# Key projections of two blocks ahead of the values, and the softmax ahead of the first group's row work, in a cross-attention and expert kernel

## Chip, cores and metric

The kernel runs on one core of one Trainium2 chip. The metric is the device time of one execution in microseconds (us); smaller is better. In what follows PE is the matrix engine, DVE the vector engine, ACT the scalar engine, POOL the GpSimd engine and SP the engine whose queue issues nearly all DMA transfers.

## The reference

```python
x = x + xattn(layernorm(x), ctx[:, :100], ctx[:, :100])      # 32 batches of 100 rows, width 512, 16 heads of 32, causal
x = x + ffn(layernorm(x))
# xattn: q = X WQ^T, k = C WK^T, v = C WV^T; softmax(q k^T / sqrt(32)) v; times Wfc^T, plus bfc
# ffn: shared expert  gelu(x Ws_g^T) * (x Ws_u^T) Ws_d^T  over all 3200 rows, plus 16 experts,
#      each with the 12 best rows of each batch (top_k of softmax(x gate_w^T)), scaled and scattered back
```

Only the first 100 context rows of a batch matter, since the mask is causal. All is float32. Each float32 operand is split into a rounded high part and a low rest, and one product is three matmuls (high by high, high by low, low by high); `mm3` issues them.

## The kernel before

The 3200 rows lie in order of batch. **Keys and values** are projected in nine blocks j of 2, 2, 3, 3 ... tiles of 128 rows. `kproj(j, c)` gives the keys of a block for one quarter c of the width in 12 matmuls, `kkeep` copies them from PSUM to a ring of SBUF tiles on ACT (L200) and stores them to DRAM from SP (L201). `vproj(j, i)` gives the values of one tile, `vkeep` copies and stores them (L183, L185). Both projections use one PSUM ring of two tiles (`ps_kv`, which `qproj` and later the first group's matmuls use too), so a projection waits until the last but one result has been copied out. The SBUF ring `kk` has two tiles, so a copy waits until the last but one store has landed.

**The prologue** is written out by hand: loads of the weights of keys (four `split_wc(0, c)`), values (`split_w(1, d)`) and queries (`split_wc(2, c)`), of the context of blocks 0, 1 and 2 (`ctx_load`, `ctx_split`), and of four tiles of x with their layer norm (`x_load`, `x_stats`, `x_norm`) and their transposes on PE (`x_turn`). Each split is a cast on ACT (L100, L134) and a subtraction on DVE or POOL (L101, L135). Its order on PE is: four keys of block 0, two values of block 0, first key of block 1, `x_turn`, three keys of block 1, first value of block 1.

**The units.** 32 units follow, one for each quarter of the width of four batches. Unit u projects q (`qproj`), takes the scores and softmax of unit u - 1 (`scores`, `sm_max` on DVE, `sm_sub` on POOL, `sm_exp` on ACT, `sm_sum` on DVE, `sm_mul` on POOL), and turns the probabilities of unit u - 2 on PE (`p_turn`, L277, copied by `p_keep`, L282) and multiplies them by the values (`values`, L292, copied by `y_keep`). `p_turn`, `values`, `x_turn` and `turn` share a second PSUM ring of two tiles (`ps_ms`). In most units one more key and value tile is projected.

**The last three units** (`end` = 0, 1, 2, that is units 29, 30 and 31) have no keys and values left. In their place stands the row work of the feed-forward's first group of three tiles (class `Prep`): `split_y` (ACT L826, DVE L827), `fc` (12 matmuls), `bias` (L837), `add` (L846), `stats`, `rsqrt` on POOL (L859, L860), `norm`, `turn` (four transposes, L885) and `logits`. `F.chunk_load` loads a chunk of expert weights (768 KB, L615) into a ring of two raw tiles, and `chunk_split` splits it (ACT L626, DVE L627); the chunk 0 is split in three parts. Then come the tail (scores, softmax, transposes and values of the last unit) and `F.begin`, the first gate and up matmuls of the shared expert, and the long feed-forward stage.

On each engine the order of instructions is that of the program's text within the hand-ordered region. Where that region meets the feed-forward's, a scheduler merges both, so the order there is read from the built program: in the tail ACT casts the last part of chunk 0, then takes the second `sm_exp`, then casts chunk 1, then does the first two `p_keep`, then casts chunk 2, then does the other two.

Of the kernel before, what the change touches and what calls it, by code (L numbers as in the profile page):

```python
# [11 lines left out]
ALU = mybir.AluOpType  # L12
# [6 lines left out]
NC4 = D // 128  # L19
# [7 lines left out]
KMAX = 384  # L27
KS = 1
FC_AT = 9
BUF = dict(cr=4, raw=6, cx=8, x=5, v=2, kk=2, kt=3, vt=2, q=3, p=5, pt=5, y=2, pj=2, sc=1, tr=2)  # L30
GROUPS = [3, 2, 2, 3, 3, 3, 3, 3, 3]
GMAX = 384
NSLOT = B * CAP
# [6 lines left out]
def f32(ap):  # L40
    return ap.bitcast(F32)
# [18 lines left out]
def attention(tc, K, F):  # L60
    nc = tc.nc
    with ExitStack() as ctx, ExitStack() as kvctx:
# [40 lines left out]
        def load_w(w, dk):  # L103
            r = raw.tile([128, D], F32, name="raw")
            nc.sync.dma_start(r, K.wA[w, :, dk, :])
            return r

        def split_w(w, dk, r):
            split(WH[w][:, dk, :], WL[w][:, dk, :], r)

        def load_wc(w, c):
            r = raw.tile([128, D], F32, name="raw")
            nc.sync.dma_start(r.rearrange("p (d n) -> p d n", d=NC4),
                              K.wA[w, :, :, c * 128:(c + 1) * 128])
            return r

        def split_wc(w, c, r, eng=None):
            cs = slice(c * 128, (c + 1) * 128)
            split(WH[w][:, :, cs], WL[w][:, :, cs], r.rearrange("p (d n) -> p d n", d=NC4), eng)
# [3 lines left out]
        def ctx_load(j, d):  # L123
            t0, n = KSTART[j] * 128, KVB[j] * 128
            cr = crp.tile([128, KMAX], F32, name="cr")
            nc.sync.dma_start(cr[:, 0:n], K.ctxT[d, :, t0:t0 + n])
            cur["cr", j, d] = cr
# [11 lines left out]
        def x_load(sb, b):  # L139
            if b == 0:  # L140
                cur["xh", sb] = xnp[sb % 2].tile([128, NC4, SB], FR, name="xnh")
                cur["xl", sb] = xnp[sb % 2].tile([128, NC4, SB], FR, name="xnl")
            xt = xp.tile([S, D], F32, name="xt")
            r0 = (sb * 4 + b) * S
            nc.sync.dma_start(xt, K.x[r0:r0 + S, :])
            cur["x", sb, b] = xt

        def x_stats(sb, b):
            st = stp.tile([S, 6], F32, name="bst")
            mv = stp.tile([S, 2], F32, name="mv")  # L150
            rs = stp.tile([S, 1], F32, name="rs")
            nc.vector.bn_stats(st, cur["x", sb, b])
            nc.vector.bn_aggr(mv, st)
            nc.gpsimd.tensor_scalar(rs, mv[:, 1:2], EPS, None, ALU.add)
            nc.gpsimd.tensor_tensor(rs, rs, K.nhalf[0:S, 0:1], ALU.pow)
            cur["mv", sb, b] = mv, rs
# [40 lines left out]
        def kkeep(j, c, pk):  # L197
            t0, n = KSTART[j] * 128, KVB[j] * 128
            kk = kkp.tile([128, KMAX], F32, name="kk")
            nc.scalar.copy(kk[:, 0:n], pk[:, 0:n])  # L200
            nc.sync.dma_start(K.kD[:, c, t0:t0 + n], kk[:, 0:n])  # L201
# [104 lines left out]
        def prologue():  # L306
            nc.gpsimd.dma_start(mask, K.mask)
            wk = [load_wc(0, 0)]
            for d in range(NC4):
                ctx_load(0, d)  # L310
            wk += [load_wc(0, c) for c in range(1, NC4)]
            wv = [load_w(1, 0), load_w(1, 1)]
            split_wc(0, 0, wk[0])
            for d in range(NC4):
                ctx_split(0, d, nc.vector)
            wv.append(load_w(1, 2))
            for b in range(2):
                x_load(0, b)
            p0 = kproj(0, 0)
            split_wc(0, 1, wk[1])  # L320
            wv.append(load_w(1, 3))
            kkeep(0, 0, p0)
            p0 = kproj(0, 1)
            split_wc(0, 2, wk[2])
            split_wc(0, 3, wk[3])
            for b in range(2, 4):
                x_load(0, b)
            for d in range(NC4):
                ctx_load(1, d)
            wq = [load_wc(2, 0), load_wc(2, 1)]  # L330
            kkeep(0, 1, p0)
            p0 = kproj(0, 2)
            split_w(1, 0, wv[0])
            split_w(1, 1, wv[1])
            kkeep(0, 2, p0)
            p0 = kproj(0, 3)
            split_w(1, 2, wv[2])
            x_stats(0, 0)
            split_w(1, 3, wv[3])
            wq += [load_wc(2, 2), load_wc(2, 3)]  # L340
            kkeep(0, 3, p0)
            p0 = vproj(0, 0)
            x_norm(0, 0)
            x_stats(0, 1)
            x_stats(0, 2)
            x_norm(0, 1)
            x_stats(0, 3)
            for d in range(NC4):
                ctx_split(1, d, nc.vector)
            x_norm(0, 2)  # L350
            x_norm(0, 3)
            vkeep(0, 0, p0)
            p0 = vproj(0, 1)
            split_wc(2, 0, wq[0])
            for d in range(NC4):
                ctx_load(2, d)
            x_load(1, 0)
            vkeep(0, 1, p0)
            for c in range(NC4):
                kkeep(1, c, kproj(1, c))  # L360
                if c == 0:
                    for b in range(4):
                        x_turn(0, b)
                if c:
                    split_wc(2, c, wq[c], nc.gpsimd)
                    ctx_split(2, c - 1)
                else:
                    kload(0)
            ctx_load(3, 0)
            vkeep(1, 0, vproj(1, 0))  # L370

        with tc.manual_schedule():
            prologue()
            for u in range(NU):
# [26 lines left out]
                if end == 0:  # L401
                    F.chunk_load()
                    F.chunk_load()
                if end == 1:
                    pr.add(0)
                    pr.stats(0)
                    pr.rsqrt(0)
                if end == 2:
                    pr.add(2)
                    pr.stats(2)  # L410
                    pr.rsqrt(1)
                    pr.store(0)
                if a is not None:
# [8 lines left out]
                if end == 0:  # L422
                    pr.bias(0)
                if end == 1:
                    pr.bias(1)
                if end == 2:
                    pr.rsqrt(2)
                if mine:
                    qkeep(u, qproj(u))
                if a is not None:  # L430
                    sm_exp(a, 0)
                if end == 0:
                    pr.split_y(0)
                if back is not None:
                    p_turn(back, 0)
                    p_turn(back, 1)
# [1 line left out]
                    p_keep(back, 1)  # L438
                if xs:
                    x_stats(sb + 1, c)  # L440
                if end == 0:
                    pr.split_y(1)
                if end == 2:
                    pr.norm(1)
                if a is not None:
                    sm_exp(a, 1)
                    sm_sum(a, 0)
# [3 lines left out]
                if end == 1:  # L451
                    pr.fc(1)
                    pr.norm(0)
                    F.chunk_split(0, 0)
                if end == 2:
                    pr.turn(0)
                    pr.norm(2)
                if mine and c == 1:
                    vload(sb)
                if back is not None:  # L460
# [7 lines left out]
                    sm_sum(a, 1)  # L468
                    sm_mul(a, 1)
                if end == 0:  # L470
                    pr.split_y(2)
                if end == 1:
                    pr.bias(2, nc.vector)
                    pr.add(1)
                    pr.stats(1)
                if mine and jn in blocks:
# [11 lines left out]
                if end == 1:  # L488
                    pr.fc(2)
                if end == 2:  # L490
                    F.chunk_split(0, 1)
                    pr.turn(1)
                if back is not None:
                    values(back)
                if end == -1:
# [14 lines left out]
            for b in range(4):  # L510
                p_turn(last - 1, b)
                p_keep(last - 1, b)
            pr.turn(2)
            values(last - 1)
            for hb in range(2):
                sm_exp(last, hb)
                sm_sum(last, hb)
                sm_mul(last, hb)
                if hb == 0:
                    y_keep(last - 1)  # L520
                    pr.logits()
                    F.chunk_split(0, 2)
            pr.store(2)
            F.chunk_split(1)
            scctx.close()
            F.open_gu()
            F.begin(pr.done())
            pr.tokens()
            for b in range(4):
                p_turn(last, b)  # L530
                p_keep(last, b)
            F.begun()
            values(last)
            y_keep(last)
# [2 lines left out]
class FeedForward:  # L537
# [77 lines left out]
            self.nc.sync.dma_start(self.raws[n], self.K.wE[n // NFC, n % NFC])  # L615
            self.asked += 1

    def chunk_split(self, n, part=None):
        nc, f = self.nc, n % NFC
        if n not in self.sw:  # L620
            hl = self.wp[f].tile([128, 2, 3 * D], FR, name=f"whl{f}")
            self.sw[n] = hl[:, 0, :], hl[:, 1, :]
        h, l = self.sw[n]
        r = self.raws[n]
        cs = slice(0, 3 * D) if part is None else slice(part * D, (part + 1) * D)
        nc.scalar.copy(h[:, cs], r[:, cs])  # L626
        nc.vector.tensor_tensor(l[:, cs], r[:, cs], f32(h[:, cs]), ALU.subtract)  # L627
        if part in (None, 2):
            self.chunk_load()

# [421 lines left out]
```

## Time and profile before

| what | value |
|---|---|
| time of one execution | 1749.06 us median of 3 (1748.99 to 1749.1) |
| the profiled execution | 1750.64 us, its span from first to last instruction 1748.8 us |
| mean granted PE clock | 0.987 |
| busy in the span | PE 1698.7 us, DVE 885.7, ACT 681.2, POOL 445.0 |
| 0 to 41 us (prologue) | PE busy 32.1 us of 41 |
| 41 to 330 us (units to 27) | PE busy 277.4 us of 289, clock 0.98 |
| 330 to 385 us (units 28 to 31) | PE busy 47.2 us of 55, clock 0.88 |
| 385 to 400 us (tail) | PE busy 13.0 us of 15, clock 0.89 |
| 400 to 1740 us (feed-forward) | PE busy 1329 us of 1340, clock 1.00 |

Times of single instructions below are in microseconds from the span's start. In a timeline line the first number is the start, the second the duration of the group; `x4` counts its instructions, and the bracket says how long the engine had sat idle before and what released it. A line of the windows gives a stretch, its length, the busy time of PE with its number of matmuls, the granted clock (1.00 is full, 0.50 half), and the load of the DMA engines.

### The profile page before, as it was taken

What the parts mean: (1) busy time and instruction counts of PE and PEld (TensorE: products, weight loads), DVE (VectorE), ACT (ScalarE), POOL (GpSimd) and SP (SyncE); (2) the same over time, 40 slices, a digit from 0 to 9 for tenths busy, and PEclk for the clock granted to TensorE, in tenths of its full rate; (3) what the DMA queues carried; (4) which work ended last, traced back from release to release, by engine and by line L of the source; (5) the groups of instructions that cost most, each with busy time, mean ns of one, the idle gap of its engine ahead of it and who ended that gap; (6) DMA issues with size and microseconds to landing.
All of it is one profiled execution on the core that took longest, in us unless ns stands there. A gap on an engine that the chain in (4) does not pass through costs nothing.

```text
span 1748.8 us, 27994 instructions
## 1 busy us (share of the span) xinstructions
PE 1698.7 (97%) x11072; PEld 1559.6 (89%) x11072; DVE 885.7 (51%) x2118; ACT 681.2 (39%) x1086; POOL 445.0 (25%) x399
## 2 busy tenths in 40 slices
PE   7999999989999999999999999999999999999996
PEld 6888888878888999999889999999999999999996
DVE  4877777775333333333454444444444444444431
ACT  4555555543112111211234444444444444444431
POOL 3777777661111011101020111110111111011111
PEclk9999999989999999999999999999999999999998
DMA  7444443534111101102154555554555554555531
GB/s 211 136 137 155 131 131 118 164 109 134 70 63 59 55 31 67 61 19 73 46 185 142 163 141 153 158 158 148 148 159 147 163 153 143 156 162 137 137 88 18
DMA packets 82995, 211.13 MB, mean 121 GB/s; under 512 B 9489, under 2 KB 35842, under 8 KB 82864
## 3 DMA queue, kind: packets, MB, share of 16 engines
q1 hardware_dynamic: 71792, 183.87, 32.2%
q0 software_dynamic: 10784, 25.21, 7.9%
q8 instruction: 87, 1.43, 0.3%
q14 instruction: 44, 0.36, 0.1%
q10 hardware_dynamic: 288, 0.27, 0.0%
HBM read 163.71 MB, written 45.60 MB: 120 GB/s over the span
## 4 chain that ended last, share of the span: by engine, by line
PE 91%; DVE 3%; DMA 2%; POOL 2%; ACT 1%; issue 1%; SPq 0%; POOLq 0%; ACTq 0%; DVEq 0%
PE gu L55 46%; PE dn L55 23%; PE kv L55 10%; PE m L55 3%; PE ms L277 2%; PE sc L236 2%; PE ms L292 1%; POOL p L256 1%; DMA big<-yD 1%; PE m L779 1%; DVE p L247 1%; PE ms L167 1%; DVE xt L161 1%; DMA kD<-kk 1%; PE m L894 1%
## 5 line engine op out<-in xcount | busy, mean ns | idle before, releaser
L55 PE MATMUL gu<-xh,whl 128*128 128x384 f32 (+1 forms) x3200 | 645.0, 333 | 1.3 <-ACT g L654 1.3
L55 PEld LDWEIGHTS gu<-xh,whl 128*128 128x128 f32 x3200 | 559.0, 188 | 18.8 <-ACT g L654 1.5
L55 PE MATMUL dn<-whl,hh 128*128 128x512 f32 x1168 | 372.4, 400 | 0.0
L627 DVE TENSOR_TENSOR whl<-wraw,whl 128x1536 fp32r<-128x1536 f32 (+1 forms) x138 | 242.1, 1755 | 241.9 <-ACT whl L626 241.8
L55 PE MATMUL gu<-xl,whl 128*128 128x384 f32 (+1 forms) x1600 | 338.1, 333 | 0.0
L55 PEld LDWEIGHTS gu<-xl,whl 128*128 128x128 f32 x1600 | 280.8, 188 | 0.0
L655 DVE TENSOR_TENSOR g<-g,gu 128x384 f32<-128x384 f32 (+1 forms) x200 | 108.7, 544 | 319.1 <-PE gu L55 316.8
L658 ACT CAST hh<-g 128x384 fp32r<-128x384 f32 (+1 forms) x200 | 100.9, 505 | 431.8 <-DVE g L655 431.8
L55 PEld LDWEIGHTS dn<-whl,hh 128*128 128x128 f32 x1168 | 213.3, 189 | 37.3
L626 ACT CAST whl<-wraw 128x1536 fp32r<-128x1536 f32 (+1 forms) x138 | 201.4, 1460 | 105.3 <-PE dn L55 103.4
L55 PE MATMUL dn<-whl,hl 128*128 128x512 f32 x584 | 230.9, 395 | 0.0
L654 ACT ACTIVATE g<-gu 128x384 f32<-128x384 f32 (+1 forms) x200 | 96.7, 484 | 312.5 <-PE gu L55 312.4
L793 POOL DMA_INDIRECT out_dram<-x,isl x48 | 77.5, 1615 | 365.5 <-ACT x L792 355.8
L659 DVE TENSOR_TENSOR hl<-g,hh 128x384 fp32r<-128x384 f32 (+1 forms) x200 | 111.8, 559 | 114.2 <-ACT hh L658 114.2
L768 POOL DMA_INDIRECT big<-xnD,isl x48 | 48.7, 1015 | 422.5 <-PE m L779 351.8
L55 PEld LDWEIGHTS dn<-whl,hl 128*128 128x128 f32 x584 | 109.8, 188 | 25.9
L271 POOL TENSOR_TENSOR p<-p,sm 100x800 f32<-100x800 f32 x64 | 101.2, 1583 | 51.0 <-DVE sm L266 36.6
L256 POOL TENSOR_TENSOR p<-p,mx 100x800 f32<-100x800 f32 x64 | 96.5, 1528 | 49.7 <-DVE mx L247 49.7
L837 POOL TENSOR_TENSOR x<-x,bfc 128x512 f32<-128x512 f32 x24 | 44.4, 1875 | 248.4 <-DMA x<-x 248.4
L247 DVE CUSTOM_DVE_ANT_0 p<-sc,mask 100x100 f32<-100x100 f32 x512 | 95.6, 257 | 16.6 <-PE sc L236 16.6
L265 DVE TENSOR_REDUCE sm<-p 100x8 f32<-100x800 f32 x64 | 62.7, 980 | 14.1 <-ACT p L260 14.1
L260 ACT ACTIVATE p<-p 100x800 f32<-100x800 f32 x64 | 56.2, 879 | 17.3 <-POOL p L256 17.3
(138 smaller groups left out, 1650.7 us busy)
## 6 DMA issues: line engine op xcount, KB each, us to landing
wraw<-wE SPq DMA_DIRECT2D x136, 768.0 KB, 4.5
xt<-x SPq DMA_DIRECT2D x32, 200.0 KB
vD<-vt SPq DMA_DIRECT2D x25, 256.0 KB, 2.1
kt<-kD SPq DMA_DIRECT2D x32, 200.0 KB, 4.9
v<-vD SPq DMA_DIRECT2D x8, 800.0 KB
x<-x SPq DMA_DIRECT2D x25, 256.0 KB, 5.1
xnD<-xn SPq DMA_DIRECT2D x25, 256.0 KB, 2.0
out_dram<-x SPq DMA_DIRECT2D x25, 256.0 KB, 2.2
```

Of the source, the lines that this page charges most:

```text
L55: r = nc.tensor.matmul(out, t[0][a], t[1][b], start=(first and i == 0), stop=(last and i == n - 1))
L247: nc.vector.tensor_tensor_reduce(out=p[:, bb, h, :], in0=sc[:, h, cs], in1=mask, scale=ISCALE, scalar=NEG, op0=ALU.add, op1=ALU.max, accum ...
L256: nc.gpsimd.tensor_tensor(pv, pv, mx[:, :, None].to_broadcast([S, 8, S]), ALU.subtract)
L265: nc.vector.tensor_reduce(sm, pv, AX.X, ALU.add)
L271: nc.gpsimd.tensor_tensor(pv, pv, sm[:, :, None].to_broadcast([S, 8, S]), ALU.mult)
L626: nc.scalar.copy(h[:, cs], r[:, cs])
L627: nc.vector.tensor_tensor(l[:, cs], r[:, cs], f32(h[:, cs]), ALU.subtract)
L654: nc.scalar.activation(g[:, 0:t], pg[:, 0:t], AF.Gelu)
L655: nc.vector.tensor_tensor(g[:, 0:t], g[:, 0:t], pu[:, 0:t], ALU.mult)
L658: nc.scalar.copy(hh[:, 0:t], g[:, 0:t])
L659: nc.vector.tensor_tensor(hl[:, 0:t], g[:, 0:t], f32(hh[:, 0:t]), ALU.subtract)
L793: ins = nc.gpsimd.indirect_dma_start(out=self.K.out, out_offset=bass.IndirectOffsetOnAxis(ap=r.isl[:, i:i + 1], axis=0), in_=o, in_offset= ...
```

## The change

It has three parts. **Rings:** the key copies get a ring of four tiles instead of two, the loaded key tiles (`kt`) two instead of three. **Prologue:** PE does the four keys of block 0, the four keys of block 1, the two values of block 0, `x_turn`, the first value of block 1. To that end the context of block 1 is loaded ahead of the last two value weights and of all x tiles, and its split stands beside the keys of block 0; the x tiles are loaded behind the second key store; the splits of the value weights and the statistics of x stand between the keys of block 1. One of the three context splits of block 2 in the prologue goes from POOL to DVE.

**Last units and tail:** in units 30 and 31 the softmax's maxima come ahead of `add`, `stats` and `rsqrt` of tiles 0 and 2; the three `split_y` move behind the softmax and the transposes of unit 29; `bias(2)` goes from DVE to POOL; the splits of chunk 0's first two parts move from units 30 and 31 to unit 31 and the tail, with their subtractions on POOL; `logits` goes behind `F.begin`; the split of chunk 1 goes behind the last unit's transposes.

In the built program the merged order in the tail is a different one: ACT casts the last part of chunk 0, then chunk 2, then copies the logits, then does the four `p_keep` of the last unit, and then casts chunk 1.

```diff
-BUF = dict(cr=4, raw=6, cx=8, x=5, v=2, kk=2, kt=3, vt=2, q=3, p=5, pt=5, y=2, pj=2, sc=1, tr=2)
+BUF = dict(cr=4, raw=6, cx=8, x=5, v=2, kk=4, kt=2, vt=2, q=3, p=5, pt=5, y=2, pj=2, sc=1, tr=2)
...
-            wv.append(load_w(1, 2))
-            for b in range(2):
-                x_load(0, b)
+            for d in range(NC4):
+                ctx_load(1, d)
             p0 = kproj(0, 0)
             split_wc(0, 1, wk[1])
-            wv.append(load_w(1, 3))
+            wv.append(load_w(1, 2))
             kkeep(0, 0, p0)
             p0 = kproj(0, 1)
             split_wc(0, 2, wk[2])
-            split_wc(0, 3, wk[3])
-            for b in range(2, 4):
-                x_load(0, b)
-            for d in range(NC4):
-                ctx_load(1, d)
-            wq = [load_wc(2, 0), load_wc(2, 1)]
+            wv.append(load_w(1, 3))
             kkeep(0, 1, p0)
             p0 = kproj(0, 2)
-            split_w(1, 0, wv[0])
-            split_w(1, 1, wv[1])
+            split_wc(0, 3, wk[3])
+            for b in range(4):
+                x_load(0, b)
+            wq = [load_wc(2, 0), load_wc(2, 1)]
+            ctx_split(1, 0, nc.vector)
             kkeep(0, 2, p0)
             p0 = kproj(0, 3)
...
+            for d in range(1, NC4):
+                ctx_split(1, d, nc.vector)
             kkeep(0, 3, p0)
+            for c in range(NC4):
+                p0 = kproj(1, c)
+                split_w(1, c, wv[c])
+                kkeep(1, c, p0)
+                if c == 0:
+                    wq.append(load_wc(2, 2))
+                    kload(0)
+                if c == 1:
+                    wq.append(load_wc(2, 3))
+                x_stats(0, c)
+                if c:
+                    x_norm(0, c - 1)
...
             vkeep(0, 1, p0)
-            for c in range(NC4):
-                kkeep(1, c, kproj(1, c))
...
+            for b in range(4):
+                x_turn(0, b)
             ctx_load(3, 0)
-            vkeep(1, 0, vproj(1, 0))
+            p0 = vproj(1, 0)
+            for d in range(NC4 - 1):
+                ctx_split(2, d, nc.vector if d == 0 else nc.gpsimd)
...
                 if end == 1:
+                    pr.add(0)
+                    pr.stats(0)
+                    pr.rsqrt(0)
                     pr.bias(1)
                 if end == 2:
+                    pr.add(2)
+                    pr.stats(2)
                     pr.rsqrt(2)
...
                 if end == 0:
-                    pr.split_y(2)
+                    for i in range(pr.nt):
+                        pr.split_y(i)
                 if end == 1:
-                    pr.bias(2, nc.vector)
+                    pr.bias(2)
...
+            y_keep(last - 1)
+            F.chunk_split(0, 2)
             pr.store(2)
-            F.chunk_split(1)
             scctx.close()
             F.open_gu()
             F.begin(pr.done())
+            p_turn(last, 0)
+            p_turn(last, 1)
+            pr.logits()
...
             pr.tokens()
-            for b in range(4):
-                p_turn(last, b)
-                p_keep(last, b)
+            F.chunk_split(1)
             F.begun()
```

## The prediction, made before the changed kernel was run

> **What bounds the kernel now.** I read the page first, then the waits of PE, then stretches of one clock step each, then the timelines of ACT and SP in the two places that the change touches.
>
> ```profile
> PE 1698.7 (97%) x11072; PEld 1559.6 (89%) x11072; DVE 885.7 (51%) x2118; ACT 681.2 (39%) x1086; POOL 445.0 (25%) x399
> ...
> PE 91%; DVE 3%; DMA 2%; POOL 2%; ACT 1%; issue 1%; SPq 0%; POOLq 0%; ACTq 0%; DVEq 0%
> ```
>
> PE is busy for 97% of the span and makes 91% of the chain that ended last. The change adds and removes no matmul. So its whole effect is the time in which PE waits, and the time in which PE runs at half clock. The waits of PE over the span name what can be won:
>
> ```profile
> PE ms L167 <- DVE xt L161: 10.4, 7, 1.7
> ...
> PE ms L277 <- ACT pt L282: 4.1, 3, 2.3
> PE ms L885 <- ACT pt L282: 3.7, 1, 3.7
> ...
> PE kv L55 <- ACT kk L200: 3.0, 2, 2.2
> ```
>
> The last is the prologue's key ring (2.2 us and 0.7 us). The second and third lie in units 29 to 31. The first is `x_turn` in units without a value tile; nothing here touches it. ACT's own rows in the prologue show why the key copies are late: the store two tiles back had not landed.
>
> ```profile
> 15.66 0.37 ACT L200 COPY kk<-kv 128x256 f32<-128x256 f32 x1 [2.50 <-DMA kD<-kk]
> 20.99 0.37 ACT L200 COPY kk<-kv 128x256 f32<-128x256 f32 x1 [3.92 <-DMA kD<-kk]
> ```
>
> The windows, cut where the clock changes, show what an idle gap costs beside itself:
>
> ```profile
> 78.38:81.79 3.41, 1.82 (x58) 1.00 0.57 180
> 81.79:85.21 3.42, 3.42 (x28) 0.50 0.33 120
> ...
> 341.20:344.62 3.42, 2.17 (x17) 1.00 1.03 355
> 344.62:348.03 3.41, 2.34 (x15) 1.00 1.04 320
> ...
> 365.10:368.51 3.41, 0.91 (x10) 1.00 0.00 0
> 368.51:371.92 3.41, 1.78 (x8) 0.50 0.20 77
> 371.92:375.34 3.42, 3.22 (x44) 0.50 0.00 0
> ```
>
> After a window of 3.41 us with 1.82 us busy (1.90 at 252.46), the next runs at half clock; 2.17 and 2.34 busy kept it full. At half clock a 128x512 matmul takes 0.425 us instead of 0.23, so a half window of dense work costs 1.6 us. Units 30 and 31 and the tail have five such windows (368.51 to 382.16, and 395.82 to 399.23).
>
> **Part 1, the prologue.** Before, `qproj` of unit 0 starts at 35.38. Now, in turn:
> - The fourth key ends at 13.84, as before: it waits for nothing that moves by more than 0.1.
> - Block 1's context now follows the second value weight (cast at 12.54, after waiting for its landing). Between the two key stores that ACT waited for, SP's queue moved two x tiles, four context tiles, two query weights and a store, 1552 KB, in 20.9 - 15.6 = 5.3 us, so 290 KB per us. 512 KB then land by 14.3; with a cast of 0.41 and a subtraction of 0.42, key 5 runs from 14.0 to 15.7 with a short stall. The wait of 2.2 us is gone, and the half clock behind it (16.94 to 20.35, 1.6 us).
> - Keys 6 to 8, at 1.44 each (12 matmuls, 29.74 to 31.18): 20.0.
> - The first value needs key 7's PSUM tile copied, and that copy needs the *third* key store landed. The x tiles and two query weights now stand ahead of that store on SP. Counted up, 4768 KB are queued up to and with it; up to the second store before it were 4640 KB of the same transfers, landed at 20.9. So it lands at 21.4, the copy ends at 21.7, and PE has idled 1.7 us. A ring of four takes away one wait and moves the other.
> - Two values at 2.76 (32.62 to 35.38) end at 27.2, four `x_turn` at 2.5 together (25.71 to 28.23, their own stall included) at 29.7, the value of block 1 at 32.5. That is 2.9 us earlier. If the 1.7 us fall into one window, half clock takes back 1.6; if the store lands 1 us later as well, 0.3 is left. I take half a chance of half clock: **-2.1**, between -2.9 and -0.3.
>
> On SP the x loads move behind two stores; they land by 20, and the last norm is done before `x_turn` at 27. SP still stands at `kt` until key 5's store has landed (4.7 us before); what queues behind it is block 2's context, needed at 41. The smaller `kt` ring costs nothing: its slot is read by the scores of the unit before, done when SP comes there. DVE's extra 128x384 split (at most 1.0, POOL's row at L135) lies beside `vproj`.
>
> **Part 2, units 1 to 28.** Nothing is edited, but the 1.65 us idles at `x_turn` shift against the clock's windows. Four of six (78, 164, 209, 252 us) now lie inside one window and cost 1.5 each. Shifted, it may be two to six: -3 to +3, taken as **0**.
>
> **Part 3, units 29 to 31, against before's times.** In unit 29 ACT now does exp (343.61), two `p_keep` (0.87), exp (345.2), two `p_keep`, and only then `split_y`: the first cast ends at 347.3 where it ended at 345.2. `fc(0)` starts at 347.45 instead of 346.33, and PE has idled 3.2 us instead of 2.3 inside some 4 us. That drops one of the two windows above under 1.82, so half clock follows, 1.2 to 1.6. The `yl` subtractions, hidden then as now, are done before `fc` needs them. In unit 30 `fc(1)` waits 0.85 us, since `add(0)`, which frees its PSUM tile, now stands behind 16 maxima (2.96 us). Against that, unit 31's maxima no longer wait for `bias`, two `add` and `stats`: they start at 365.0 to 365.4, before at 365.19. So the gain in the softmax pays for what unit 29 lost. `turn(0)` starts at 369.5 to 369.9 (369.70 before), the second gap of 1.8 us follows (the PSUM slot waits for `turn(0)`'s subtraction), and the half clock over transposes, scores and values stays as it was. The last part of chunk 0 is split 0.3 to 0.6 earlier than before; were the clock to stay full, the same steps give 381.3 instead of 386.06, so -4.7. POOL's two new subtractions (1.29 each, its row for 128x512 at L101) and `bias(2)` (1.29 to 1.57) stand behind both `sm_sub` or end 2 us before the next: nothing.
>
> **Part 4, the tail,** decides. When chunk 0's last part is split, SP issues chunk 2's load into its slot:
>
> ```profile
> 386.06 0.33 SPq L615 DMA_DIRECT2D wraw<-wE  x1
> ...
> 390.90 1.48 ACT L626 CAST whl<-wraw 128x1536 fp32r<-128x1536 f32 x1 [0.97 <-DMA wraw<-wE]
> ```
>
> From that issue to ACT's cast of chunk 2 it is 4.84 us, and to the first `dn` matmul (398.37) 12.3 us, with chunk 1 cast before. Now that cast stands on ACT ahead of the logits' copy, the four `p_keep` and chunk 1's cast, and all these wait for the load: 4.84, cast 1.38, copy 0.38, first `p_keep` 0.49 give 7.1; two more transposes at half clock (0.8 each) and `p_keep` give 9.3; chunk 1's cast 1.47 gives 10.7; then 24 matmuls, 4.2 at full clock or 7.7 at half, since PE has idled 4 us before. So 15 to 18 us, 16.0 taken. With the issue at 385.7 `dn` starts at 401.7: **+3.3** (-1 where the clock had stayed full, +5 at worst). The next chunk's loads come 8 us later than before but are needed only at 408.
>
> [...]
>
> **Sum.** -2.1 + 0 + 3.3 = +1.2. The profiled execution took 1750.64 (1.84 outside its span), 1.58 over the median of 1749.06; the difference is the same on either, so 1750.3 on the median. About 0.2%, 3.5 us, is what a measurement of this kernel can tell from no change.
>
> **Rivals.**
> - *No measurable change* (the forecast, 0.50): gain in the prologue, given back in the tail: 1746 to 1752.5. It holds the case that the rings don't do what they are for: if the third store lands at 23.5, the prologue gives 0 and the time is 1752.4.
> - *Slower* (0.29): ACT's queue behind chunk 2's load. The wait is there whatever the clock does, 3.7 us by the middle of its range, 5.5 with half clock through all 24 matmuls. It decides when issue to `dn` passes 16.5 us with a prologue of -0.3, or 18.3 with -2.1 (12.3 + 3.5 + the prologue's gain + 0.4 for the earlier issue). Price: -0.3 + 4.8, 1753.6. For it: ACT's order in the built program. Against: two of its terms rest on a half clock.
> - *Faster* (0.21): the gap of 3.69 us before `turn(0)` goes, the clock stays full from unit 29 to the tail, `dn` starts at 381.3 + 16 = 397.3 (-1.1), the prologue gives -2.9, and one idle less is punished in the loop (-1.5): 1743.6. Against: unit 29 idles more than now.
>
> The range of 8 in 10 reaches from the faster case, 1744.0, to a little over the slower one, 1754.5.
>
> **What would show it.** Right: `qproj` of unit 0 near 32.5, a key copy waiting for a store at about 21, a gap of 3 us in unit 29, ACT idle for about 4 us before chunk 2's cast, and issue to `dn` near 16. Wrong: a clock of 1.00 from 340 to 380, or chunk 1's cast ahead of chunk 2's.

## The result and the profile after

The changed kernel takes 1753.73 us (median of 20 runs, 1749.37 to 1755.08), the kernel before, run beside it, 1749.14 us (20 runs, 1747.22 to 1751.38). The ratio is 1.0024, with a 95% interval of 1.0017 to 1.0031: some 4 us slower, on the edge of the 0.2% that can be told from no change. A second measurement, told below, gave 1.0014 (1.0003 to 1.0025). That the change is slower is settled; whether by more or by less than 0.2% is not.

The time lies inside the predicted range and 3.4 us above the predicted value. It is outside the forecast of no measurable change (1746 to 1752.5), and it is the time of the rival "slower" (1753.6).

The profiled execution after took 1753.64 us (span 1751.9), the one before 1750.64 (span 1748.8), so 3.0 us of the 4.6 between the medians can be looked up in the two traces. The other 1.6 is that the profiled execution of before was itself 1.5 over its median.

From the page of the changed kernel, the busy times and the chain that ended last:

```profile
PE 1697.2 (97%) x11072; PEld 1558.3 (89%) x11072; DVE 884.3 (50%) x2116; ACT 680.5 (39%) x1086; POOL 445.9 (25%) x401
...
PE 90%; DVE 2%; POOL 2%; DMA 2%; issue 1%; ACT 1%; SPq 0%; POOLq 0%; ACTq 0%; DVEq 0%
```

PE has the same 11072 matmuls and still makes 90% of the chain. The difference is in its waits. In the list of PE's waits over the span (total, times, longest) two lines matter:

```profile
PE ms L277 <- issue: 5.0, 1, 5.0
...
PE kv L55 <- ACT kk L200: 2.6, 1, 2.6
```

The second is the key ring: before it was two waits of 2.2 and 0.7, now it is one of 2.6. It stands ahead of the first value, where ACT waits for a key store before it copies the seventh key (a row of ACT's timeline, then one of PE's):

```profile
22.10 0.37 ACT L200 COPY kk<-kv 128x256 f32<-128x256 f32 x1 [4.03 <-DMA kD<-kk]
22.52 0.50 PE L55 MATMUL kv<-wh,cxh 128*128 128x512 f32 x1 [2.56 <-ACT kk L200]
```

The first is new. "issue" means that the profile found no semaphore for it; what it is shows on ACT. ACT's timeline in the tail (start, duration, and in brackets the idle time and its releaser):

```profile
383.04 0.62 ACT L622 CAST whl<-wraw 128x512 fp32r<-128x512 f32 x1
390.29 1.47 ACT L622 CAST whl<-wraw 128x1536 fp32r<-128x1536 f32 x1 [6.63 <-DMA wraw<-wE]
391.78 0.47 ACT L893 COPY so<-kv 16x384 f32<-16x384 f32 x1
392.28 0.89 ACT L282 COPY pt<-ms 100x400 f32<-100x400 f32 x2
```

ACT stands 6.63 us in front of chunk 2's cast. The load that it waits for could not be issued before DVE had done its last subtraction of chunk 0 (rows of DVE and of SP's queue):

```profile
384.26 1.21 DVE L623 TENSOR_TENSOR whl<-wraw,whl 128x512 fp32r<-128x512 f32 x1
385.53 0.33 SPq L611 DMA_DIRECT2D wraw<-wE  x1
```

Behind chunk 2's cast in ACT's queue are the copy of the logits and the first two `p_keep`, whose inputs PE had finished by 387.84 and 386.4. They start at 391.78 and 392.28 in these rows, behind the end of that cast at 391.76. The next two transposes need the PSUM tiles that `p_keep` frees, so PE stands too. PE's timeline:

```profile
386.98 0.86 PE L890 MATMUL kv<-xl,gw 128*64 128x384 f32 x4
392.87 1.54 PE L277 MATMUL ms<-ident,p 100*100 100x100 f32 x8 [5.03 <-issue]
...
401.71 0.63 PE L55 MATMUL dn<-whl,hh 128*128 128x512 f32 x2
```

Half clock is on record behind these gaps. In the windows of 3.41 us, cut at the clock's steps (stretch, length, PE's busy time and matmuls, granted clock, DMA share, GB/s) a whole window is empty in the tail, and two of half clock come after it; after 2.37 us of idle in unit 29 comes one:

```profile
344.03:347.45 3.42, 1.04 (x9) 1.00 1.05 417
347.45:350.86 3.41, 3.41 (x9) 0.50 0.92 322
...
388.41:391.82 3.41, 0.00 (x0) 1.00 0.50 199
391.82:395.23 3.41, 2.36 (x23) 0.50 0.16 20
395.23:398.65 3.42, 3.33 (x35) 0.50 0.53 215
```

The two traces, stretch by stretch. "T" is the first matmul behind the transposes and values of unit 30: that of the logits before (382.41), that of the gate after (381.28). From T to the first `dn` both kernels do the same PE work in another order.

| stretch | before | after | difference |
|---|---|---|---|
| start to `qproj` of unit 0 | 35.38 | 35.22 | -0.16 |
| to the scores of unit 1 | 14.53 | 15.06 | +0.53 |
| to the scores of unit 28 | 289.43 | 288.95 | -0.48 |
| unit 29, to the scores of unit 29 | 10.78 | 13.40 | +2.62 |
| unit 30, to the scores of unit 30 | 11.31 | 12.00 | +0.69 |
| unit 31, to T | 20.98 | 16.65 | -4.33 |
| T to the first `dn` | 15.96 | 20.43 | +4.47 |
| first `dn` to the last matmul's end | 1336.78 | 1336.51 | -0.27 |

The half clock falls elsewhere in each execution (from 345 to 385 us the mean clock was 0.83 in `before`, 0.87 in `after`, and 1.00 in `after_again`, which has the text of `after`), so the profiled executions of the runs below are needed beside this pair. The tail's loss holds in them: T to the first `dn` takes 19.2 to 21.3 us in the five executions that have the order of the changed tail (this one, `c_only`, `store34`, `y_early`, `after_again`), and 16.0 to 16.7 in the three that have the order of before (`before`, `p_only`, `ring_only`). The sum of the units and the tail spreads more: from the scores of unit 28 to `dn` it is 59.5 to 63.3 us in the four executions with the changed last units and tail (without `y_early`), and 57.9 to 60.0 in three with those of before.

### The profile page after: what moved, and what is told of

It reads as the page before. It is cut to its first block, busy times and chain, and to the rows that moved or that the text cites. A ratio compares the mean times of both kernels' runs of the same rounds, so it can differ in the third digit from the quotient of the medians.

```text
span 1751.9 us, 27984 instructions
## 1 busy us (share of the span) xinstructions
PE 1697.2 (97%) x11072; PEld 1558.3 (89%) x11072; DVE 884.3 (50%) x2116; ACT 680.5 (39%) x1086; POOL 445.9 (25%) x401
## 4 chain that ended last, share of the span: by engine, by line
PE 90%; DVE 2%; POOL 2%; DMA 2%; issue 1%; ACT 1%; SPq 0%; POOLq 0%; ACTq 0%; DVEq 0%
PE gu L55 46%; PE dn L55 23%; PE kv L55 9%; PE m L55 4%; PE ms L277 2%; PE sc L236 2%; POOL p L256 2%; PE ms L292 1%; PE m L775 1%; DVE p L247 1%; DVE xt L161 1%; PE ms L167 1%; DMA big<-yD 1%; PE m L890 1%; PE m L881 1%
## 5 line engine op out<-in xcount | busy, mean ns | idle before, releaser
L277 PE MATMUL ms<-ident,p 100*100 100x100 f32 x512 | 56.7, 254 | 10.1 <-issue 5.0
```

Of the source, the lines that this page charges most:

```text
L277: nc.tensor.transpose(tp[0:S, h, 0:S], p[:, b % 2, h, :], K.ident[0:S, 0:S])
```

## The experiments

All ratios are to the kernel before, run in the same batch (its medians were 1750.07, 1750.79 and 1750.10 in the three batches).

| run | median us (n) | ratio (95%) |
|---|---|---|
| `p_only` | 1749.74 (11) | 0.9991 (0.9982 to 1.0000) |
| `c_only` | 1753.37 (11) | 1.0017 (1.0008 to 1.0026) |
| `a_hook` | 1752.24 (11) | 1.0008 (0.9999 to 1.0017) |
| `store34` | 1751.64 (11) | 1.0006 (0.9996 to 1.0016) |
| `a_hook2` | 1751.84 (12) | 1.0005 (0.9993 to 1.0018) |
| `y_early` | 1750.69 (12) | 1.0000 (0.9991 to 1.0010) |
| `best2` | 1743.68 (7) | 0.9967 (0.9954 to 0.9979) |
| `best3` | 1746.83 (12) | 0.9979 (0.9970 to 0.9987) |
| `ring_only` | 1746.60 (8) | 0.9979 (0.9969 to 0.9989) |
| `t_hook2` | 1747.35 (12) | 0.9993 (0.9979 to 1.0007) |
| `best4` | 1743.35 (6) | 0.9971 (0.9959 to 0.9983) |
| `after_again` | 1753.21 (9) | 1.0014 (1.0003 to 1.0025) |

**The halves alone.** `p_only` is the kernel before with the change's `BUF` line and its whole `prologue()`:

```diff
-BUF = dict(cr=4, raw=6, cx=8, x=5, v=2, kk=2, kt=3, ...
+BUF = dict(cr=4, raw=6, cx=8, x=5, v=2, kk=4, kt=2, ...
...
```

> The kernel before with the change's rings and prologue alone; units 29 to 31 and the tail as before. Theory of the tail (the slowdown is ACT's queue held by chunk 2's load between begin and the first dn): the prologue gives nothing, because the third key store lands at 22 and half clock follows, and unit 0 loses 0.5 more at x_turn; qproj of unit 0 starts at 35.2, the scores of unit 0 at 41.3, time within 1 us of the kernel before (1748.5 to 1750.1). Rival (the prologue shifts the loop's idles against the clock's windows, so that more of them are punished, and that is most of the 4.6 us): 1752 or more.

`c_only` is the changed kernel with the line and the prologue of before:

```diff
-BUF = dict(cr=4, raw=6, cx=8, x=5, v=2, kk=4, kt=2, ...
+BUF = dict(cr=4, raw=6, cx=8, x=5, v=2, kk=2, kt=3, ...
...
```

> The changed kernel with the rings and the prologue of before; units 29 to 31 and the tail of the changed kernel. Theory of the tail: nearly all of the loss is here, 1752.5 to 1754; from the load of chunk 2 to the first dn 16 us. Rival (prologue and clock windows carry the loss): 1749 to 1751.

The first gave -0.09%, the second +0.17%. In the trace of `p_only`, `qproj` of unit 0 starts at 35.56 and the scores of unit 0 at 41.61 (35.38 and 40.77 before). In that of `c_only`, from the load of chunk 2 (385.34) to the first `dn` (401.69) it is 16.35 us. So the loss is in the last units and the tail, and the prologue is not what slows the kernel. (The profiled execution of `p_only` was the slowest of its eleven, 3.1 us over their median; the times, not its trace, carry this.)

**The whole once more**, to see whether the halves add up:

> The changed kernel once more, beside the other three on one chip. The parts run alone gave -0.09% for the prologue and +0.17% for units 29 to 31 with the tail, together +0.08%, and the whole +0.24%. If the two parts are separate, this run comes near +0.1% (1.0005 to 1.0016); if they make each other worse, near +0.24% again (1.0018 or more).

It gave +0.14%. This lies in the band for separate parts, but its interval (0.03 to 0.25) holds both cases; whether the two halves make each other worse stays open.

**ACT's order.** `a_hook` moves chunk 2's split of the first feed-forward job from behind job step 0 to a hook that `hidden` calls after its gelu:

```diff
         nc.scalar.activation(g[:, 0:t], pg[:, 0:t], AF.Gelu)
+        if hook:
+            hook()
...
             if g == 0:
-                for f in range(NFC - 2):
+                self.hook = lambda: self.chunk_split(2)
+                for f in range(1, NFC - 2):
```

> The changed kernel, and only ACT's cast of chunk 2 is moved behind the second gelu, so that nothing of the last unit waits on ACT for chunk 2's load. Theory of the tail: ACT copies the logits at 387.9, does the four p_keep until 390.2, casts chunk 1 until 391.7; the first dn starts near 396 instead of 401.7, time 1747.5 to 1749.5, 4 to 6 us under the changed kernel. Rival (the loss is chunk 1's cast behind the last unit, or the prologue): dn later than 399 and a time of 1752 or more.

By both its numbers (`dn` at 402.49, 1752.24 us) the outcome is that of the rival; by the stretch that the theory is about, it is that of the theory. From the gate's first matmul to the first `dn` it is 15.3 us (387.16 to 402.49) instead of 20.4, but the gate started 5.9 us later, so this run alone does not decide. The edit had a side effect: with chunk 2's split gone from their way, the second group's loads of y and x and its two `bias` moved ahead of the tail (the x loads to 348.72, in unit 29), and in unit 30 POOL waited for a load that stands behind two chunks, with two `sm_sub` behind it. POOL's timeline:

```profile
360.38 2.49 POOL L837 TENSOR_TENSOR x<-x,bfc 128x512 f32<-128x512 f32 x2 [6.90 <-DMA x<-x]
362.82 3.00 POOL L256 TENSOR_TENSOR p<-p,mx 100x800 f32<-100x800 f32 x2
```

`a_hook2` puts those loads into the hook, behind the split:

```diff
-                self.hook = lambda: self.chunk_split(2)
+                q = self.prep(1)
+                self.hook = lambda: [c() for c in (lambda: self.chunk_split(2), q.load_y, ...)]
```

> The changed kernel with ACT's cast of chunk 2 behind the second gelu, as in the run before, and the second group's y and x loads kept behind it, so that POOL's and SP's order stay those of the changed kernel (in the run before they moved ahead into unit 30, and POOL stood 6.9 us at one of them). Theory (ACT's queue held by chunk 2's load costs the tail some 5 us): begin near 381.3 as in the changed kernel, the first dn 15 to 15.6 us behind it instead of 20.4, so near 396.6; time 1747.5 to 1750. Rival (what the run before saved in the tail is owed to its later begin, by which time the load had landed anyway): dn 19 us or more behind begin, and no more than 1.5 us saved.

Between the theory and the rival: 1751.84, over the theory's range, and 17.69 us from the gate (380.16) to `dn` (397.85). The 6.63 us on ACT are gone. But two smaller gaps are left, 1.1 us (the first two `p_keep` stand behind the logits' copy) and 0.9 us (chunk 1's cast behind the last `p_keep`), and in this execution two windows of half clock lay over the 24 matmuls that follow (the first four took 1.65 us, four behind them at 397.15 0.85). The list of PE's waits from 380 to 398 of this run:

```profile
PE ms L277 <- issue: 1.1, 1, 1.1
PE gu L55 <- ACT whl L622: 0.9, 1, 0.9
```

`t_hook2` therefore also puts chunk 1's split back ahead of `F.begin`:

```diff
             pr.store(2)
+            F.chunk_split(1)
             scctx.close()
...
-            F.chunk_split(1)
             F.begun()
```

> The changed kernel with both orders of ACT's tail mended: chunk 2's cast behind the second gelu, and chunk 1's split ahead of begin. Theory (with chunk 2's cast moved, the logits' copy and chunk 1's cast behind the last p_keep still leave PE idle for 1.1 and 0.9 us and at half clock): begin to the first dn 15 to 15.6 us, against 17.7 with chunk 2's cast moved alone and 20.4 in the changed kernel; 3.5 to 5.5 us under the changed kernel. Rival (chunk 1's place does not matter): dn 17 us or more behind begin, 1 to 2.5 us under the changed kernel.

Confirmed: 15.24 us from the gate (379.13) to `dn` (394.37). In the time it is 0.21% (3.7 us; 5.9 between the medians) under the changed kernel of the same batch, and 0.31% by the first measurement of the changed kernel. The second chunk's gate matmuls fill the time in which ACT copies. In that stretch one wait is left, for ACT's gelu:

```profile
PE gu L55 <- ACT g L651: 1.3, 1, 1.3
```

**Unit 29.** `y_early` undoes the move of the three splits:

```diff
+                if end == 0:
+                    pr.split_y(0)
                 if back is not None:
                     p_turn(back, 0)
...
+                if end == 0:
+                    pr.split_y(1)
                 if a is not None:
                     sm_exp(a, 1)
...
                 if end == 0:
-                    for i in range(pr.nt):
-                        pr.split_y(i)
+                    pr.split_y(2)
```

> The changed kernel with the three split_y of unit 29 back where the kernel before has them. Theory (the later split costs unit 29 its start of fc(0) and a window of half clock, and unit 31's maxima follow the scores at once, so what unit 29 loses reaches the end): fc(0) 1 us earlier against the scores of unit 28, no half clock in unit 29, scores of unit 30 2 to 3 us earlier, begin 2 to 3 us earlier; time 1750.5 to 1752. Rival (the softmax of unit 31 or a transfer sets the end of unit 31 whatever unit 29 does, as the lag of 3.2 us that was given back by the scores of the last unit suggests): begin within 0.7 us of the changed kernel's, 1753 to 1754.

The theory holds with a smaller size: 1750.69; from the scores of unit 28 to those of unit 30 it is 23.45 us instead of 25.40, and T comes 1.95 us earlier against the same mark. `fc(0)` is 0.67 earlier, not 1. A window of half clock still fell on it (eight transposes took 1.49 us at 346.26 and 0.85 at 343.25), so that part of the expectation was wrong: a gap of 2.16 us is left, at the PSUM tile of the transposes.

**The third key store.** `store34` reorders SP's queue:

```diff
-            for b in range(4):
-                x_load(0, b)
-            wq = [load_wc(2, 0), load_wc(2, 1)]
             ctx_split(1, 0, nc.vector)
             kkeep(0, 2, p0)
+            for b in range(4):
+                x_load(0, b)
...
             kkeep(0, 3, p0)
+            wq = [load_wc(2, 0), load_wc(2, 1)]
```

> The changed kernel, and only the loads of the four x tiles move behind the third key store on SP, and those of two query weights behind the fourth. Theory (the third store's landing, late because six transfers stand ahead of it, is what holds the first value projection): the store lands by 18, PE idles under 0.7 us ahead of the first value, no half clock follows, qproj of unit 0 at 32.3 to 33.3 instead of 35.2; time 1.5 to 3 us under the changed kernel, 1751 to 1752. Rival (the x tiles then come late and x_turn waits for their norm instead): qproj of unit 0 still at 34.5 or later, and no gain.

Confirmed in the trace: `qproj` of unit 0 at 32.68. The time, 1751.64, is 2.1 under the first median of the changed kernel and 1.6 under the second, both of other batches; with these intervals the times alone don't show the gain. ACT's timeline shows that key 7's copy no longer waits, and that the wait for the fourth store is left for key 8, behind PE's back:

```profile
18.59 0.37 ACT L200 COPY kk<-kv 128x256 f32<-128x256 f32 x1 [0.55 <-ACT wh L100]
...
21.94 0.37 ACT L200 COPY kk<-kv 128x256 f32<-128x256 f32 x1 [2.46 <-DMA kD<-kk]
```

**The ring alone.** This is the change's first line and nothing else, so the loaded key tiles (`kt`) go from three to two with it; the two sizes were not run apart.

```diff
-BUF = dict(cr=4, raw=6, cx=8, x=5, v=2, kk=2, kt=3, ...
+BUF = dict(cr=4, raw=6, cx=8, x=5, v=2, kk=4, kt=2, ...
```

> The kernel before with the rings' sizes alone (four key tiles, two loaded key tiles); its order unchanged. Theory (the ring is what was needed, and the new order of the prologue only moves the wait to the third store): PE's waits for the key copies ahead of the two first values, 2.2 and 0.7 us, go; qproj of unit 0 at 32.5 to 34 instead of 35.4; 1 to 2.5 us under the kernel before. Rival (the value weights' splits, which queue behind the same copies on ACT, are late as well): qproj at 35 or later, no change.

Confirmed. At -0.21% it looks better than the ring with the new order (-0.09%), but that was another batch and the intervals overlap, so this is not shown by the times. `qproj` of unit 0 starts at 33.14 and the scores of unit 0 at 38.53, against 35.38 and 40.77. PE's waits from 13 to 41 us of this run:

```profile
PE kv L55 <- ACT wh L100: 1.2, 1, 1.2
PE ms L167 <- DVE xnl L101: 0.8, 1, 0.8
PE kv L55 <- ACT kk L200: 0.3, 1, 0.3
PE kv L55 <- DVE wl L101: 0.2, 1, 0.2
```

Of the key copies' 3.0 us, 0.3 are left; the value weights' cast took 1.2 of the place. In the old order of PE the fifth key comes after two values, and ACT's copy of it, at 23.72, waits for no store. So in this trace a larger ring was enough, and eight keys in a row ask for a third store too early.

**Together.** `best3` keeps the last units and ACT's order of before, with the change's ring and prologue, `store34` and the hook of `a_hook2`:

> The kernel before (its units 29 to 31 and the order of its tail) with the change's rings and prologue, the x loads behind the third key store and two query weights behind the fourth, and chunk 2's cast behind the second gelu. Theory: the prologue 2 to 2.7 us, the tail 1.5 to 2.4 us (the cast of chunk 2 and the wait ahead of it no longer stand between the last unit's copies): 1744.5 to 1747. Rival (in the order of before nothing in the tail waits for that cast but work that is late anyway): 1747 to 1748.

1746.83, inside the theory's range and 0.2 short of the rival's; from the load of chunk 2 (383.42) to `dn` (394.22) it is 10.8 us instead of 12.3. Its ratio is also that of the ring alone (0.9979), so the times don't show that the new prologue order and the hook add anything to that one line. `best2` is the changed kernel with all four mends (those of `store34` and `y_early`, and the two of `t_hook2`):

> The changed kernel with four mends: the x loads behind the third key store and two query weights behind the fourth, split_y early in unit 29, chunk 1's split ahead of begin, and chunk 2's cast behind the second gelu. Theory (the three losses are separate and add up: 2.5 us in the prologue, 2.5 in unit 29, 5 to 7 in the tail): 1741 to 1746, faster than both kernels. Rival (half clock and transfers eat most of it): 1747 or more.

1743.68, the fastest with `best4`, 0.33% under the kernel before, which makes it some 0.5% under the changed one. The windows over units 30 and 31 up to 385 us, first of the kernel before, then of `best2`:

```profile
345.00:385.00 40.00, 34.44 (x367) 0.83 0.33 113
```

```profile
345.00:385.00 40.00, 35.24 (x436) 1.00 0.37 123
```

69 more matmuls are on record in the same 40 us: the clock is never halved in them, and PE is busy 0.8 us longer. T comes at 372.56 and `dn` at 387.85; from the scores of unit 28 to `dn` it is 51.8 us, against 59.0 before and 62.5 after (57.9 to 60.0 and 59.5 to 63.3 over the executions named above).

**Unit 0.** The prologue's new order had a cost that the prediction didn't name: from `qproj` to the scores of unit 0 it is 6.05 us in the changed kernel and 5.39 before. PE waits 0.5 us for the normed x tile of the next unit; its reciprocal root stands on POOL behind the splits that were moved. POOL's timeline of the changed kernel:

```profile
34.03 2.02 POOL L135 TENSOR_TENSOR cxl<-cr,cxh 128x384 fp32r<-128x384 f32 x2 [4.40 <-ACT cxh L134]
36.02 2.54 POOL L101 TENSOR_TENSOR wl<-raw,wh 128x512 fp32r<-128x512 f32 x2
38.53 0.21 POOL L154 TENSOR_SCALAR rs<-mv 100x1 f32<-100x1 f32 x1
```

`best4` is `best2` with all of block 2's context splits of the prologue on DVE:

```diff
-                ctx_split(2, d, nc.vector if d == 0 else nc.gpsimd)
+                ctx_split(2, d, nc.vector)
```

> The run with four mends, and all three context splits of block 2 in the prologue on DVE instead of one. Theory (the four x tiles of unit 1 wait for POOL's reciprocal root behind two context splits and two weight splits, and that is the 0.5 to 1.1 us that unit 0 lost): from qproj of unit 0 to the scores of unit 0 6.2 us or less instead of 6.85; time 0.5 us less than the run with four mends, too little to be told from it by the times. Rival (DVE's two more splits delay the statistics by as much): 6.8 us again.

5.93 us instead of 6.85, as the theory said; the time (1743.35) can't be told from that of `best2`.

## Why the prediction was right or wrong

**The tail: right, to 0.2 us.** Predicted were 16.0 us from the issue of chunk 2's load to the first `dn`, issued at 385.7, and `dn` at 401.7. Measured: 16.18, 385.53 and 401.71. That it is ACT's order, and not chunk 1's late cast alone, is shown by `a_hook2` (14.0 us, 383.88 to 397.85) and `t_hook2` (11.7, 382.65 to 394.37): each of the two casts moved takes some 2.2 us away, though the half clock also lay differently in these executions (the first four of the 24 matmuls took 1.65 us in `a_hook2`, 0.88 in `t_hook2`). The terms came as written: the cast started 4.76 us behind the issue (4.84 predicted), the 24 matmuls began at 10.9 (10.7) and took 5.3, the middle way that the prediction had taken between 4.2 and 7.7. That the agreement is as close as 0.2 us is luck: the other executions with this tail took 14.9 to 16.9 us. Off was the sign "ACT idle for about 4 us": it stood 6.6, from 383.66 on, 1.9 before the load was issued. The sum counts from the issue, so this doesn't enter it.

**Units 29 to 31: the marks nearly right, the clock not.** Predicted were `fc(0)` at 347.45 with a window of half clock, a wait of 0.85 for `fc(1)` and `turn(0)` at 369.5 to 369.9; measured 347.27 with the window, 0.65 and 370.21. That half clock would stay over unit 31 "as it was" is what failed: two of its windows instead of four. PE idled 1.5 us before `turn(0)` and not 3.7, but that this is the whole reason is not shown: before, the windows from 371.92 and 375.34, with 0.2 and 0.06 us of idle, were followed by half clock too. T came 1.13 us earlier. It brought little: the load of chunk 2 hangs on DVE's last subtraction of chunk 0 and came 0.53 us earlier (385.53 for 386.06), and everything behind hung on the load. `after_again` shows it more strongly, and the prediction's own sign of being wrong with it: there the clock was 1.00 from 345 to 385 and T came at 377.80, but the load was issued at 382.14 and `dn` started at 399.07, 16.9 us behind it. The rival "faster" saw this mechanism; `best2` is that rival with the tail mended.

**The prologue: its term is the step that failed in this execution**, -0.16 instead of -2.1. Each link stood: the eighth key ended at 19.97 (20.0 predicted), the first value waited for the third store, half clock was a coin's toss. But the copy ended at 22.5, not 21.7, PE idled 2.56 and not 1.7, and half clock did follow, as it did in `p_only` behind 2.95 and in `a_hook` behind 2.70, but not in `y_early` behind 2.46. Across the seven executions that have this prologue text, `qproj` of unit 0 started between 32.88 and 35.56, 34.22 on the mean; of the old one there are two, 35.38 and 37.30. That mean is 1.2 under the profiled execution of before and 2.1 under the mean of the two, so the size may have been fair over executions, as far as two of the old prologue can tell, and `p_only` is not slower. What was missing is unit 0 (+0.53): the part on moved steps looked at SP's queue and at DVE, and not at what POOL does behind the splits.

**Units 1 to 28** were taken as 0, with ±3: -0.48 measured, three windows punished instead of four.

**The sum** in the profiled executions was to be +1.2, and is +3.0: +1.94 from the prologue, +0.53 from unit 0, -0.48 from the loop, +0.15 from the rest up to `dn`, and -0.27 behind it. By the ratios, though, the two halves alone make some +1.4 us (-1.6 and +3.0) and the whole +2.5 and +4.2 in its two measurements; what the difference is stays open. The rival "slower" had the mechanism, though neither of its two conditions was met: it asked for over 16.5 us from issue to `dn` with a prologue of -0.3, and 16.18 were enough since unit 0 gave the rest. Its price of +4.5 is that of the medians (+4.6) and not of the traces (+3.1), so that it met the time is in part luck.

**The clock in the rows.** In the trace after, 1.65 and 2.37 us of idle in one window (367.93 and 344.03) were each followed by half clock; 1.57 us, at 862.86, was not. The rows give no one threshold: before, a window with 1.90 us busy (252.46) was followed by half clock, and after, one with 1.84 (862.86) was not. Before, the idle of 1.64 us ahead of 79.97 lay in one window (78.38, 1.82 busy), and half clock followed; that of 1.68 ahead of 123.50 lay over two (119.34 and 122.75, 2.49 and 2.66 busy), and it did not. The loop of units 1 to 28, whose text is the same, has four windows of half clock before and three after.

## What to carry to other kernels

Where a cast waits for a transfer, ask what stands behind it on its engine: one cast that stood too early on ACT emptied PE for 5 us by way of a PSUM ring, and with that and three smaller waits mended a loss of 4 us became a gain of 6. Try a larger ring before a new order: the ring alone removed the waits that the order then brought back. And mend all gaps of a stretch or expect little, since here a gap of 1.6 to 2 us was followed by a window of half clock, some 1.5 us more (that of 1.64 in one window before), or by none (that of 1.68 over two windows), and a part's value shows only beside its neighbours.

## What was not expected of the hardware

- The same code spreads by 3 to 10 us between executions (1748.6 to 1756.2 in nine runs of the changed kernel, 1743.9 to 1754.3 in twelve of `t_hook2`), and the granted clock goes with it (in `t_hook2` 0.992 at 1743.98 us and 0.987 at 1754.27). By an estimate from these two runs, the 0.005 between their clocks is five windows of 3.41 us at half clock (0.005 of some 1747 us, over half of 3.41), each some 1.5 us by the prediction's 0.425 for 0.23, so some 8 of the 10 us; that it hangs on where the idles of 1.6 us fall was not shown. One profile's difference of 3 us is therefore no verdict; the medians and the marks inside the trace are.
- Landings in the prologue move by more than 1 us between executions: the old prologue's first value started at 16.08 in `before` and at 17.97 in `c_only`, both waiting for the same key store.
- In `a_hook` an x tile's load issued at 348.72, behind two chunks of 768 KB issued at 345.24, let POOL go on at 360.38 only, over 11 us later.
